# Forward substitution steps on VectorE moved behind the addition to x, in a gated delta-net and feed-forward kernel on one Trainium2 core

## Chip, core and metric

The kernel runs on one core of one Trainium2 chip. A core has five engines that run side by side and wait for each other through semaphores: PE (TensorE, matmuls; its weight loads are listed apart as PEld), DVE (VectorE), ACT (ScalarE), POOL (GpSimd) and SP (SyncE, which here issues the DMAs). The metric is the device time of one execution in microseconds (us), the median of several. A profile is one execution that the hardware profiler recorded.

## What is computed

The input x has 4 sequences of 1024 tokens of width 256. Two layers follow one another, each as x + layernorm(layer(layernorm(x))): a gated delta-net attention with 32 value heads of width 128 (16 query/key heads, each for two value heads), and a feed-forward layer whose weights are looked up in a table of 16 values. Nearly all the time goes into the first. Cut to what matters, for each head and each chunk of 64 tokens:

```python
mixed = silu(conv4(x @ W_qkv))                 # q, k, v; q and k are then normalised
A = -(k_beta @ k.T * decay) * strict           # 64x64, strictly lower triangular
Tm = solve_triangular(eye - A, eye)            # its inverse, by forward substitution
u, kcd = Tm @ v_beta, Tm @ (k_beta * exp(g))
# over the 16 chunks in order, St is the state (128x128):
v_new = u - kcd @ St
out = (q * exp(g)) @ St + attn @ v_new
St = St * exp(g_last) + (k * exp(g_last - g)).T @ v_new
```

The output of a head is then normalised, gated with silu(x @ W_z) and projected with W_out.

## The kernel before

**Tiling.** Two sequences and one chunk make a tile of 128 rows (`p` is the pair of sequences, 0 or 1). Four heads are worked on together (a group; there are eight), and a group's 32 tiles are cut into four super-blocks of eight units. A unit is one tile with four heads. There are 256 units in 32 super-blocks. Consecutive units belong to the two pairs in turn, so the state that a unit reads was last changed two units before.

**The slots.** The order of the work is written out by hand. Each pass of the loop of line 871 is a slot: it carries one unit through the recurrence, and does a share of the work for later super-blocks and for the output of earlier units. The strings of `SLOTS` (lines 858 to 867) give the order of issue, one string for each value of `iq` from 0 to 7; I call them slot 0 to slot 7. Each word resumes a generator up to its next `yield`:

- `A` and `B` (`channel`, line 389): the projection and the four-tap convolution of a channel tile of v (A) and of q or k (B). PE writes PSUM (L422), ACT takes the first tap (L436), DVE adds the other three into the tile `cv` (L439), ACT applies silu (L443). The convolution's later parts are put off by a few words through a list of due work (`go`, line 821). A step `v` doesn't count in that list.
- `N0`, `N1`, `N2`, `O3`, `O4`, `J` (`step`, line 657): the recurrence of a unit. N0 transposes v (L670) and scales it into x0 (L674). N1 multiplies k and q with the state (`pkqs`, L683), and **adds to x** on DVE (L694, four instructions; the profile calls the tile x). N2 applies the diagonal inverse to it on PE (`px`, L703), makes `xs` (ACT, L708) and `yg` (DVE, L711), and has POOL decay the state (L720). In the next slot O3 multiplies with the attention (`po`, L703) and adds on DVE (`core`, L727), J squares on ACT (L732), and O4 multiplies into `pu` (L740) and **adds to the state** S on DVE (L747). So a slot's O3, J and O4 belong to one unit and its N1 and N2 to the next one.
- `Z`, `T`, `U` (`project_out`, line 768): the gate `pz` on PE (L142), its silu `zs` on ACT (L781), two multiplications of `zs` on POOL (L783, L785), a transpose and `pout` on PE (L789, L796), and an addition `ac` on DVE (L801).
- `n` (`norms`), `r` and `q` (`rms`, with three small DVE instructions at L753 to L762, and `roots`), `s` (`scores`: POOL L529, L530 and L536, ACT L533, PE `kkq` L545, DVE L555), `b` (`build`).
- After each O4, POOL also does a piece of the feed-forward layer's table lookup (`lut_pieces`, L300 and L304).
- `v1`, `v2`: one or two **steps of the forward substitution** (`invert`, line 563; lines 897 to 900). The inverse of the 32x32 diagonal blocks of a super-block (128 blocks, one to a partition) takes 31 steps of two DVE instructions, a product `rank` (L579) and a subtraction from `v` (L580). Step j works on (j+1)(31-j) elements a partition: 31 at both ends, 256 in the middle. A first call of the generator only loads `lb` and clears `v`; the last one also stores `v` to DRAM. The substitution of a super-block starts in slot 4 and runs through 5, 6, 7, 0 and 1; what is left in slot 2 is drained there.

```python
    for j in range(BS - 1):
        w = BS - 1 - j
        sh = [P, j + 1, w]
...
        V.tensor_tensor(t, bc(v[:, 0 : j + 1, j : j + 1], sh), bc(lb[:, j : j + 1, j + 1 :], sh), ALU.mult)
        V.tensor_tensor(v[:, 0 : j + 1, j + 1 :], v[:, 0 : j + 1, j + 1 :], t, ALU.subtract)
```

**What the engines share.** The PSUM tiles come from two rings. One has two buffers of two banks (`psum2`), taken in turn by A's `pp`, `pu` and B's `pp`, so that a slot's `pu` takes the buffer that B's `pp` of the slot before held, and waits until DVE has read it out (L439). The other has four banks (`psum`) for everything else. Each engine takes its instructions in the order of issue. The two instructions of a step have both inputs in SBUF; L694, L747, L711, L727, L555 and L439 have one input in PSUM.

Of the kernel before, what the change touches and what calls it, by code (L numbers as in the profile page):

```python
# [14 lines left out]
B, S, HID = 4, 1024, 256  # L15
# [48 lines left out]
def delta_net_ffn_kernel(  # L64
# [18 lines left out]
    V, A, G_, T_ = nc.vector, nc.scalar, nc.gpsimd, nc.tensor  # L83
# [84 lines left out]
    def layer_norm_stats(pool, src, n, tag):  # L168

        mv = pool.tile([P, n, 2], F32, tag=f"mv{tag}", name=f"mv{tag}")  # L170
        for i in range(n):
            st = pool.tile([P, 6], F32, tag=f"st{tag}", name=f"st{tag}")
            V.bn_stats(st, src(i))
            V.bn_aggr(mv[:, i, :], st)
        r = pool.tile([P, n], F32, tag=f"r{tag}", name=f"r{tag}")
        G_.tensor_scalar_add(r, mv[:, :, 1], LN_EPS)
        G_.tensor_tensor(r, r, bc(rsqrt, [P, n]), ALU.pow)
        return mv, r
# [14 lines left out]
    with tc.tile_pool(name="pre", bufs=2) as pre, tc.tile_pool(name="gates", bufs=1) as gp:  # L193
# [13 lines left out]
        for s in range(NSB):  # L207
# [4 lines left out]
            mv, r = layer_norm_stats(pre, lambda i: xt[:, i, :], SB, "a")  # L212
# [95 lines left out]
    with ExitStack() as main:  # L308
# [533 lines left out]
        def work(kind, n, *args):  # L842
# [13 lines left out]
        LQ = 2 * SB + 5  # L856
        LV = SB // 2
        SLOTS = [
            "A v1 O3 s N0 v1 T n J O4 v1 N1 Z v1 B n N2 U n s",
            "A v1 O3 N0 v1 T J v1 O4 N1 r Z v1 B N2 q s U",  # L860
            "A v1 O3 N0 v1 T J v1 O4 v1 N1 Z s v1 B N2 n U",
            "b A O3 N0 T J O4 N1 Z s B N2 U b",
            "v1 A b O3 s N0 v1 T n J O4 v1 N1 Z v1 B n N2 v1 U n s",
            "A v1 O3 N0 v1 T J v1 O4 v1 N1 r Z v1 B N2 q s v1 U",
            "A v1 O3 N0 v1 T J v1 O4 v1 N1 Z s v1 B N2 n v1 U",
            "A v1 O3 N0 v1 T J v1 O4 v1 N1 Z s v1 B N2 v1 U",
        ]

        units = [(k, u) for k in supers for u in range(SB)]
        with tc.manual_schedule(engines=COMPUTE):  # L870
            for s in range(-LQ, len(units)):
                n, i = divmod(s, SB)
# [58 lines left out]
    with tc.tile_pool(name="fw", bufs=1) as fw, tc.tile_pool(name="fs", bufs=2) as fs:  # L931
# [7 lines left out]
        for s in range(NSB):  # L939
# [6 lines left out]
            mv, r = layer_norm_stats(fs, lambda i: acb[:, i, :], SB, "b")  # L946
# [3 lines left out]
            mv, r = layer_norm_stats(fs, lambda i: xt[:, i, :], SB, "c")  # L950
# [32 lines left out]
            mv, r = layer_norm_stats(fs, lambda i: acb[:, i, :], SB, "d")  # L983
# [57 lines left out]
```

## Time and profile before

| | |
|---|---|
| time, median of 3 runs | 4435.06 us (4429.75 to 4438.18) |
| the profiled execution | 4434.46 us, of it a span of 4432.7 us |
| busy in the span: PE, PEld | 91%, 65% |
| busy in the span: DVE, ACT, POOL | 79%, 60%, 47% |
| granted PE clock, mean | 0.968 |
| L579 `rank`, 992 instructions | 468.2 us, 472 ns each |
| L580 `v`, 992 instructions | 555.0 us, 559 ns each |
| POOL L783, L785 (256 each), L720 (224) | 1041, 1283, 1947 ns each |

In a line of a timeline stand the start and the duration in us, the engine, the line of the kernel, the operation, the tile written and the tiles read, the shapes, and in brackets the idle time before it with what ended it. In a table of stretches each engine's busy time stands beside the length of the stretch. The chain of waits is followed back from the last instruction, at each step to what released it or to the instruction before it on its engine.

### The profile page before, as it was taken

What the parts mean: (1) busy time and instruction counts of PE and PEld (TensorE: products, weight loads), DVE (VectorE), ACT (ScalarE), POOL (GpSimd) and SP (SyncE); (2) the same over time, 40 slices, a digit from 0 to 9 for tenths busy, and PEclk for the clock granted to TensorE, in tenths of its full rate; (3) what the DMA queues carried; (4) which work ended last, traced back from release to release, by engine and by line L of the source; (5) the groups of instructions that cost most, each with busy time, mean ns of one, the idle gap of its engine ahead of it and who ended that gap; (6) DMA issues with size and microseconds to landing.
All of it is one profiled execution on the core that took longest, in us unless ns stands there. A gap on an engine that the chain in (4) does not pass through costs nothing.

```text
span 4432.7 us, 79363 instructions
## 1 busy us (share of the span) xinstructions
PE 4021.3 (91%) x26664; PEld 2876.3 (65%) x26664; DVE 3514.5 (79%) x6641; ACT 2646.0 (60%) x6573; POOL 2069.1 (47%) x1752
## 2 busy tenths in 40 slices
PE   3679999999999999999999999999999999995888
PEld 3456766676767766677667676776766666673444
DVE  4788888888888888888888888889888888861442
ACT  2466666666666666666666666666666666662111
POOL 2545554655555555554455555555453334331221
PEclk7899999999999999999999999999999999997999
DMA  3444444544454444444444445444444444432110
GB/s 94 114 116 110 106 120 118 133 117 114 129 135 125 118 121 132 114 116 127 126 130 118 115 127 135 125 116 118 126 119 117 123 126 120 102 84 72 36 33 19
DMA packets 1052418, 492.70 MB, mean 111 GB/s; under 512 B 729824, under 2 KB 951152, under 8 KB 1052016
## 3 DMA queue, kind: packets, MB, share of 16 engines
q1 hardware_dynamic: 1052016, 487.64, 42.0%
q8 instruction: 216, 3.54, 0.3%
q14 instruction: 186, 1.52, 0.1%
HBM read 267.66 MB, written 219.69 MB: 110 GB/s over the span
## 4 chain that ended last, share of the span: by engine, by line
PE 59%; DVE 24%; issue 6%; ACT 6%; POOL 3%; DMA 2%; SPq 1%; DVEq 0%; POOLq 0%; ACTq 0%
PE pp L422 13%; DVE cv L439 8%; PE pout L796 7%; PE pz L142 7%; PE pkqs L683 7%; PE px L703 4%; DVE rank L579 4%; PE pu L740 4%; PE po L703 3%; PE pgu L963 3%; PE py L975 2%; DVE v L580 2%; PE kkq L545 2%; PE pto L789 2%; PE pv L670 1%
## 5 line engine op out<-in xcount | busy, mean ns | idle before, releaser
L439 DVE SCALAR_TENSOR_TENSOR cv<-pp,cw,cv 128x512 f32<-128x512 f32 x1536 | 1148.8, 748 | 356.6 <-ACT cv L436 327.2
L783 POOL TENSOR_TENSOR zs<-zs,rr 128x512 f32<-128x512 f32 x256 | 266.4, 1041 | 1586.6 <-ACT zs L781 1577.6
L436 ACT ACTIVATE cv<-pp,cw 128x512 f32<-128x512 f32 x512 | 350.7, 685 | 489.3 <-PE pp L422 489.3
L580 DVE TENSOR_TENSOR v<-v,rank 128x31 f32<-128x31 f32 (+15 forms) x992 | 555.0, 559 | 34.1
L422 PE MATMUL pp<-xnT,wq 128*128 128x262 f32 x2048 | 532.1, 402 | 43.8 <-DVE cv L439 35.1
L796 PE MATMUL pout<-wo,oT 128*128 128x256 f32 x2048 | 512.0, 395 | 8.1 <-ACT oT L791 8.1
L422 PEld LDWEIGHTS pp<-xnT,wq 128*128 128x128 f32 x2048 | 372.7, 192 | 217.1 <-issue 59.6
L422 PE MATMUL pp<-xnT,wv 128*128 128x262 f32 x2048 | 502.5, 387 | 6.1 <-DVE cv L439 6.1
L142 PE MATMUL pz<-wzs,xnT 128*64 128x512 f32 x2048 | 488.8, 598 | 4.7 <-DVE ac L801 3.8
L579 DVE TENSOR_TENSOR rank<-v,lb 128x31 f32<-128x31 f32 (+15 forms) x992 | 468.2, 472 | 24.5 <-DMA lb<-ltd 18.8
L683 PE MATMUL pkqs<-S,qku 128*64 128x256 f32 x3840 | 476.8, 387 | 4.2 <-DVE core L727 2.5
L720 POOL TENSOR_TENSOR S<-S,dkm 128x1024 f32<-128x1024 f32 x224 | 436.2, 1947 | 26.0 <-PE pkqs L683 26.0
L703 PE MATMUL px<-x,ue 128*128 128x128 f32 x2048 | 296.1, 289 | 157.5 <-issue 102.2
L703 PEld LDWEIGHTS px<-x,ue 128*128 128x128 f32 x2048 | 266.9, 196 | 258.0 <-issue 147.7
L422 PEld LDWEIGHTS pp<-xnT,wv 128*128 128x128 f32 x2048 | 381.4, 190 | 74.1 <-issue 13.4
L796 PEld LDWEIGHTS pout<-wo,oT 128*128 128x128 f32 x2048 | 388.2, 200 | 56.3 <-ACT oT L791 10.0
L683 PEld LDWEIGHTS pkqs<-S,qku 128*64 128x64 f32 x3840 | 249.2, 136 | 201.4 <-issue 51.0
L732 ACT ACTIVATE junk<-core 128x128 f32<-128x128 f32 x1024 | 318.8, 311 | 66.7 <-DVE core L727 38.4
L785 POOL TENSOR_TENSOR zs<-zs,core 128x512 f32<-128x512 f32 x256 | 328.4, 1283 | 20.1
L708 ACT ACTIVATE xs<-px 128x512 f32<-128x512 f32 x256 | 154.4, 603 | 237.5 <-PE px L703 237.4
L740 PE MATMUL pu<-yg,kt 64*128 64x256 f32 x1920 | 272.2, 402 | 15.4 <-DVE cv L439 14.0
L300 POOL TENSOR_SCALAR lt<-lx,lutb 128x344 f32<-128x344 int32 (+2 forms) x210 | 276.6, 1317 | 16.9
(166 smaller groups left out, 7081.7 us busy)
## 6 DMA issues: line engine op xcount, KB each, us to landing
qkd<-qk SPq DMA_DIRECT2D x256, 256.0 KB, 2.5
qku<-qkd SPq DMA_DIRECT2D x256, 256.0 KB, 2.9
dc<-rows_d SPq DMA_DIRECT2D x256, 128.0 KB, 3.4
ltd<-lT SPq DMA_DIRECT2D x128, 256.0 KB, 2.5
atd<-aT SPq DMA_DIRECT2D x128, 256.0 KB, 2.8
ae<-atd SPq DMA_DIRECT2D x512, 64.0 KB, 2.6
acc_d<-ac SPq DMA_DIRECT2D x256, 128.0 KB, 2.2
ac<-acc_d SPq DMA_DIRECT2D x224, 128.0 KB, 2.6
```

The costliest lines, as they stand in the source:

```text
L142: T_.matmul(ps[ab * C : (ab + 1) * C, :], lhsT=xnT[:, kc, 2 * p + ab, H + n * C : H + (n + 1) * C], rhs=rhs(kc), start=kc == 0, stop=kc == ...
L422: T_.matmul(ps[:, 2 * p : 2 * p + 2, : H + BT], lhsT=wt[:, kc, :], rhs=xnT[:, kc, 2 * p : 2 * p + 2, c0 : c0 + H + BT], start=kc == 0, sto ...
L436: A.activation(cv, ps[:, :, H : H + BT], AF.Copy, scale=cw[:, ch, H : H + 1])
L439: V.scalar_tensor_tensor(cv, ps[:, :, i : i + BT], cw[:, ch, i : i + 1], cv, ALU.mult, ALU.add)
L579: V.tensor_tensor(t, bc(v[:, 0 : j + 1, j : j + 1], sh), bc(lb[:, j : j + 1, j + 1 :], sh), ALU.mult)
L580: V.tensor_tensor(v[:, 0 : j + 1, j + 1 :], v[:, 0 : j + 1, j + 1 :], t, ALU.subtract)
L683: T_.matmul(as4(ps)[ab * C : (ab + 1) * C, two, :], lhsT=qk[:, m, j, ab, :], rhs=S_[:, ab, two, :], start=True, stop=True,)
L703: T_.matmul(as4(ps)[:, h, :], lhsT=w[:, h, :], rhs=src[:, h, :], start=True, stop=True)
L720: G_.tensor_tensor(flat, flat, bc(decay, [P, 2 * HG, P]), ALU.mult)
L740: T_.matmul(as4(pu[:, ab])[:, two, :], lhsT=kt[half, m, :], rhs=yg[half, two, :], start=True, stop=True)
L785: G_.tensor_tensor(zs, zs, k.cores.pop(u), ALU.mult)
L796: T_.matmul(pp[:, :HID], lhsT=oT[:, h, :], rhs=wo[:, h, :], start=h == 0, stop=h == HG - 1)
```

## The change

The strings of the slots alone change. No step `v` stands any more between J and O4 (slots 1, 2, 5, 6 and 7), and none between O4 and N1 (slots 0, 2, 4, 5, 6 and 7). They stand behind N1: two in slots 1, 2, 4, 5, 6 and 7, one in slot 0. In slot 4 a step that stood behind Z is one of the two. The number of steps in a slot stays, but in slot 1, which has five in place of four, so that the last of the 31 steps falls into slot 1 and no longer into slot 2. All other engines keep their order of issue, and so do all DVE instructions but the steps.

```diff
         SLOTS = [
-            "A v1 O3 s N0 v1 T n J O4 v1 N1 Z v1 B n N2 U n s",
-            "A v1 O3 N0 v1 T J v1 O4 N1 r Z v1 B N2 q s U",
-            "A v1 O3 N0 v1 T J v1 O4 v1 N1 Z s v1 B N2 n U",
+            "A v1 O3 s N0 v1 T n J O4 N1 v1 Z v1 B n N2 U n s",
+            "A v1 O3 N0 v1 T J O4 N1 v2 r Z v1 B N2 q s U",
+            "A v1 O3 N0 v1 T J O4 N1 v2 Z s v1 B N2 n U",
             "b A O3 N0 T J O4 N1 Z s B N2 U b",
-            "v1 A b O3 s N0 v1 T n J O4 v1 N1 Z v1 B n N2 v1 U n s",
-            "A v1 O3 N0 v1 T J v1 O4 v1 N1 r Z v1 B N2 q s v1 U",
-            "A v1 O3 N0 v1 T J v1 O4 v1 N1 Z s v1 B N2 n v1 U",
-            "A v1 O3 N0 v1 T J v1 O4 v1 N1 Z s v1 B N2 v1 U",
+            "v1 A b O3 s N0 v1 T n J O4 N1 v2 Z B n N2 v1 U n s",
+            "A v1 O3 N0 v1 T J O4 N1 v2 r Z v1 B N2 q s v1 U",
+            "A v1 O3 N0 v1 T J O4 N1 v2 Z s v1 B N2 n v1 U",
+            "A v1 O3 N0 v1 T J O4 N1 v2 Z s v1 B N2 v1 U",
         ]
```

## The prediction

> **What bounds the kernel now.** I read the page first, then the busy time by slot, then the timelines of one super-block. The page calls it a PE kernel.
>
> ```profile
> PE 4021.3 (91%) x26664; PEld 2876.3 (65%) x26664; DVE 3514.5 (79%) x6641; ACT 2646.0 (60%) x6573; POOL 2069.1 (47%) x1752
> ...
> PE 59%; DVE 24%; issue 6%; ACT 6%; POOL 3%; DMA 2%; SPq 1%; DVEq 0%; POOLq 0%; ACTq 0%
> ```
>
> But DVE holds 24% of the chain, and the slots differ. The stretches below run from one `po` to the next: slots 5, 6, 7 and 0 of one super-block.
>
> ```profile
> core 0: us, PE busy (x) PEld busy (x) DVE busy (x) ACT busy (x) POOL busy (x), PEclk, DMA share, GB/s
> ...
> 2041.04:2058.72 17.68, 15.06 (x83) 11.02 (x82) 17.12 (x33) 11.24 (x27) 9.57 (x9) 0.90 0.36 83
> 2058.72:2073.99 15.27, 14.10 (x99) 10.63 (x98) 14.96 (x25) 9.81 (x25) 9.91 (x9) 1.00 0.26 69
> 2073.99:2089.45 15.46, 14.11 (x99) 10.62 (x98) 15.11 (x29) 7.71 (x22) 5.49 (x4) 1.00 0.56 169
> 2089.45:2104.08 14.63, 14.63 (x96) 10.22 (x94) 12.83 (x30) 9.64 (x26) 4.56 (x4) 1.00 0.47 129
> ```
>
> In slots 5 to 7 DVE is busy for all but 0.56, 0.31 and 0.35 us, which is its gaps between instructions, and PE is idle for 2.62, 1.17 and 1.35 us. **DVE bounds these three slots.** In slot 0 PE is busy throughout. So what the change does to DVE's time decides slots 5 to 7, and not how early x comes.
>
> Slot 7, on DVE:
>
> ```profile
> 2080.16 0.42 DVE L579 TENSOR_TENSOR rank<-v,lb 128x247 f32<-128x247 f32 x1
> 2080.61 0.42 DVE L580 TENSOR_TENSOR v<-v,rank 128x247 f32<-128x247 f32 x1
> 2080.95 1.22 DVE L747 TENSOR_TENSOR S<-pu,S 128x1024 f32<-128x1024 f32 x1
> 2082.08 0.83 DVE L579 TENSOR_TENSOR rank<-v,lb 128x240 f32<-128x240 f32 x1
> 2082.95 1.35 DVE L580 TENSOR_TENSOR v<-v,rank 128x240 f32<-128x240 f32 x1
> 2084.22 1.11 DVE L694 SCALAR_TENSOR_TENSOR x<-pkqs,dkm,x 128x128 f32<-128x128 f32 x4
> 2085.26 0.67 DVE L555 TENSOR_TENSOR lT<-kkq,dc 128x512 f32<-128x512 f32 x1
> ...
> 2086.46 0.38 DVE L579 TENSOR_TENSOR rank<-v,lb 128x231 f32<-128x231 f32 x1
> 2086.87 0.40 DVE L580 TENSOR_TENSOR v<-v,rank 128x231 f32<-128x231 f32 x1
> ```
>
> POOL in the same slot, and PE:
>
> ```profile
> 2081.61 1.04 POOL L783 TENSOR_TENSOR zs<-zs,rr 128x512 f32<-128x512 f32 x1 [8.95 <-ACT zs L781]
> 2082.73 1.31 POOL L785 TENSOR_TENSOR zs<-zs,core 128x512 f32<-128x512 f32 x1
> 2084.00 2.06 POOL L720 TENSOR_TENSOR S<-S,dkm 128x1024 f32<-128x1024 f32 x1
> 2086.04 1.14 POOL L300 TENSOR_SCALAR lw<-lx,lutb 128x256 f32<-128x256 int32 x1
> ```
>
> ```profile
> 2084.77 1.13 PE L703 MATMUL px<-x,ue 128*128 128x128 f32 x8 [1.35 <-DMA ac<-acc_d]
> ```
>
> Two things are to be seen. First, `px` waits 1.35 us for x, and two steps stand ahead of x (the releaser named is not the real one; x's first quarter ends at 2084.22+0.34). Second, the step at 2082.08 takes 2.22 us where its neighbours take 0.81 to 0.87: its `rank` ends at 2082.91, 0.26 us after POOL's L783 (2082.65), and its `v` at 2084.30, 0.26 us after L785 (2084.04). **A step's instruction waits while one of these POOL instructions runs.** L694 at 1.11 us and L555 at 0.67 us run beside POOL's L720 at their usual length. They read PSUM.
>
> **The change, part by part.** No instruction is added or removed. What counts is where the steps meet POOL.
>
> *POOL's block stays where it is.* L783 follows ACT's zs, which follows ACT's silu of `cv` and `qs`; the three POOL instructions run without a gap. None of what they wait for moves in DVE's order, and the steps never stood ahead of that `cv`.
>
> *Slot 7.* The step of 2080.16 goes from ahead of S, which starts there; x follows 1.13 us behind the start of S (slot 2, where no step stands between: 2123.89 and 2125.02), so it runs from 2081.29 to 2082.40. PE's wait at `px` goes. Then come four step instructions in a row, and the block is in its first 1.04 us. The first ends at 2082.91 and the second at 2084.30, as before. The third waits for the end of L720 (2084.00 + 2.06 = 2086.06) and ends near 2086.3, the fourth 0.4 later; L555 starts near 2086.65 in place of 2085.26. DVE is **1.4 us later**: before, x and L555 filled the time of L720; now a step waits it out.
>
> *Slot 6.* The same from its rows: S from 2064.36, x to 2066.6, block from 2066.12 to 2070.59, fourth instruction to 2071.3, L555 at 2071.2 in place of 2069.80: **1.4**.
>
> *Slot 5.* S from 2047.68, x to 2049.9, block 2049.32 to 2053.67, fourth instruction to 2054.3, so 1.33 later. But behind it stands `eq` (L753), which took 0.82 us beside L720 and takes 0.16 alone: 0.67. One more step meets L536 at the end of the slot in place of another, perhaps -0.3 (estimate from steps of 0.8 and 1.6 us there). **0.4**.
>
> *What of it ends late.* 3.2 us on DVE in a super-block. PE first takes up its slack: B's last `cv` in slot 7 ended at 2088.45 + 1.53 = 2089.98, and `pu`, which needs that buffer, started at 2091.31, so 1.33 us are free; slot 0's `px` has about 1.0. I take 1.2. After that PE waits at `pu` where it waited at `px`. **2.0 us** a super-block.
>
> *Slot 1.* Here only the step ahead of O4 moves, and the last step comes over from slot 2. Before, `eq` and `rr` met the block:
>
> ```profile
> 2112.61 1.27 DVE L753 TENSOR_SCALAR eq<-n 128x8 f32<-128x8 f32 x1
> 2113.99 1.75 DVE L754 SCALAR_TENSOR_TENSOR rr<-ms,eq 128x16 f32<-128x16 f32 x1
> ```
>
> They already waited out L785 and L720 (to 2115.71). Now the two steps do, and `rr`, with the extra step of 0.4 us, comes behind: B's `cv` starts near 2117.1 in place of 2116.27, 0.85 late; its end at 2119.06 had 0.05 us to `pu` (2119.11). In slot 2, PE's `pkqs` waited for `core` behind the step that is now gone (1.43 us), which gives some 0.35 back. **0.5 us**.
>
> *At nothing:* slot 0 (the step sat alone at 0.65 us ahead of x, and POOL's block starts at 2099.44, after it either way; `px` has slack; if the cover went, 0.65 us), slot 4 (steps of 60 and 87 elements, 0.47 and 0.52 us, in a slot with 7 us of DVE idle), slots 2 and 3 (no steps left to run). The last step's store of `v`, on SP, comes a few us earlier; its readers run in slot 3. The steps issue no other DMA.
>
> *Count.* 31 super-blocks have their steps beside units. In the first of each of the eight groups the units of slots 5 and 6 have no state yet, hence no x and no L720; there only slot 7 counts, 1.4 - 1.2 = 0.2. Sum: 23 x 2.0 + 8 x 0.2 + 31 x 0.5 = 46 + 2 + 16 = 64 us on the profiled execution's 4434.5 us, which is 0.6 us from the median: **4498 us**, 1.4% slower.
>
> *A rule of the skill.* The rows show steps held by TENSOR_TENSOR on POOL, but the steps at 2086.46 and 2086.87 ran at 0.38 and 0.40 us beside L300, a TENSOR_SCALAR from 2086.04 to 2087.18. The Trainium skill, "SBUF — State Buffer", section "SBUF: two separate sides", calls the pair that VectorE and GpSimd share an exclusive lock: a VectorE instruction with two SBUF inputs and a GpSimd one that reads SBUF block each other for a whole instruction. That speaks against this change, and it would let L300 block too, which the row denies. By the rule, the fourth instruction would often wait out L300 behind L720 as well, up to 1.1 us in slots 6 and 7, an estimate of up to 50 us more. I go by the row.
>
> **Rivals.** *Faster (14%):* the steps cost no more in the new place, since POOL comes late or lets both steps in between its instructions. Then DVE's time stays and what stood between `px` and `pu` is gained, 1.2 us: 31 x 1.2 = 37 us, **4398 us**. If DVE were not the bound after all, all PE waits of slots 5 to 7 would go: 23 x 5.1 + 8 x 1.35 = 128 us, 4306 us. For it: PE does wait for x. Against: DVE's columns. It decides as soon as DVE's added time in slots 5 to 7 falls under 1.2 us, of 3.2.
>
> *No change (9%):* the added waits are about 1.2 us a super-block and the slack takes them: **4435 us**.
>
> *Much slower (12%):* no slack, as PE now waits at `pu`, at `ac` and at `cv` in turn, slot 1 in full, and a further 0.8 us from steps that meet other POOL work: 23 x 4.0 + 8 x 1.4 + 31 x 0.85 = 130 us, **4564 us**. That the change didn't do what it says can't be: the order of issue is the order on DVE.
>
> **The numbers.** The forecast (65%) spans 4465 to 4535 by its own terms (1.0 to 1.5 us a slot, slack 0.9 to 1.33). The range leaves out the faster cases and what lies beyond the much slower one: 4440 to 4565. A difference under 0.2% can't be told from none here. Faster 0.14, same 0.09, slower 0.77.
>
> **What would show it.** In the profile after: `px` without its wait in slots 5 to 7 (right for the first step); steps behind x of 1 to 2 us an instruction that end just after L783, L785 and L720, and L579 and L580 with higher means than 472 and 559 ns; L753 short; new PE waits at `pu`, `pto` or `pp` for `cv` and `yg`. I am wrong if the step instructions behind x stay near 0.4 us, or if DVE shows idle time in slots 5 to 7.

## Result and profile after

The changed kernel takes 4553.53 us (median of 4 runs, 4551.29 to 4558.39), beside 4435.91 us for the kernel before (median of 4, 4429.75 to 4438.18). The ratio is 1.0269, with a 95% interval of 1.0251 to 1.0287: **117.6 us slower**. The forecast had 64 us. The time lies inside the stated range of 4440 to 4565, but above the 4465 to 4535 that the forecast spans by its own terms, and near the rival "much slower" (130 us). The executions compared in the profiles lie 124 us apart.

The profile after, from its page: the chain that ended last, and the two groups of the steps.

```profile
DVE 43%; PE 35%; ACT 11%; issue 6%; DMA 2%; POOL 2%; SPq 1%; DVEq 0%; ACTq 0%; POOLq 0%
...
L579 DVE TENSOR_TENSOR rank<-v,lb 128x31 f32<-128x31 f32 (+15 forms) x992 | 584.3, 589 | 31.2 <-DMA lb<-ltd 23.4
L580 DVE TENSOR_TENSOR v<-v,rank 128x31 f32<-128x31 f32 (+15 forms) x992 | 581.4, 586 | 34.3 <-DVE rank L579 0.2
```

PE had 59% of the chain and DVE 24%; now DVE leads. The same 1984 step instructions took 1023.2 us together and now take 1165.7.

The timeline of a slot 7, DVE first, then POOL's block in the same slot:

```profile
2027.23 0.41 DVE L579 TENSOR_TENSOR rank<-v,lb 128x252 f32<-128x252 f32 x1
...
2028.02 1.22 DVE L747 TENSOR_TENSOR S<-pu,S 128x1024 f32<-128x1024 f32 x1
2029.15 1.12 DVE L694 SCALAR_TENSOR_TENSOR x<-pkqs,dkm,x 128x128 f32<-128x128 f32 x4
2030.19 0.69 DVE L579 TENSOR_TENSOR rank<-v,lb 128x247 f32<-128x247 f32 x1
2030.91 1.37 DVE L580 TENSOR_TENSOR v<-v,rank 128x247 f32<-128x247 f32 x1
2032.32 1.99 DVE L579 TENSOR_TENSOR rank<-v,lb 128x240 f32<-128x240 f32 x1
2034.34 0.57 DVE L580 TENSOR_TENSOR v<-v,rank 128x240 f32<-128x240 f32 x1
```

```profile
2029.57 1.04 POOL L783 TENSOR_TENSOR zs<-zs,rr 128x512 f32<-128x512 f32 x1 [10.49 <-ACT zs L781]
2030.69 1.32 POOL L785 TENSOR_TENSOR zs<-zs,core 128x512 f32<-128x512 f32 x1
2031.98 2.06 POOL L720 TENSOR_TENSOR S<-S,dkm 128x1024 f32<-128x1024 f32 x1
```

Read the ends. The first three step instructions behind x end at 2030.88, 2032.28 and 2034.31; POOL's three end at 2030.61, 2032.01 and 2034.04. Each step instruction ends 0.27 us after a POOL instruction. The third takes 1.99 us, where its like at 2027.23 takes 0.41. In the same slot on PE, with the idle time before each in brackets:

```profile
2030.09 1.05 PE L703 MATMUL px<-x,ue 128*128 128x128 f32 x8
...
2036.16 0.66 PE L670 MATMUL pv<-ident,vt 128*128 128x128 f32 x4 [0.42 <-DVE aT L555]
2038.25 0.63 PE L789 MATMUL pto<-ident,zs 128*128 128x128 f32 x4 [1.43 <-DVE yg L711]
2039.61 2.08 PE L740 MATMUL pu<-yg,kt 64*128 64x256 f32 x8 [0.73 <-DVE cv L439]
```

`px` no longer waits, but PE stands 2.58 us a little later, for `aT`, `yg` and `cv`, which DVE hands over late. Over the whole run PE's longest waits are now these, where they were for `px` (102.2 us with the releaser put down as issue, 39.0 us with ACT's cv):

```profile
PE pto L789 <- DVE yg L711: 121.1, 102, 1.9
PE pu L740 <- DVE cv L439: 84.5, 118, 2.5
```

To see where the 118 us lie, I take the time from the end of one `core` (L727) to the end of the next, by slot, from both traces: medians, and the mean of 30 of each, which holds also the super-blocks at a group's start.

| from `core` of slot | 0 | 1 | 2 | 3 | 4 | 5 | 6 | 7 | sum |
|---|---|---|---|---|---|---|---|---|---|
| before, median us | 14.50 | 14.20 | 12.12 | 16.28 | 16.57 | 16.40 | 15.64 | 15.20 | 120.92 |
| after, median us | 14.51 | 13.79 | 13.52 | 16.28 | 16.57 | 16.55 | 17.05 | 16.81 | 125.08 |
| after less before, mean us | +0.25 | -0.38 | +1.36 | -0.02 | 0.00 | +0.18 | +0.85 | +1.55 | +3.80 |

3.80 us on the mean, 31 times, is 118 us. Slots 5 to 7 give 2.58 of them, slots 1 and 2 together 0.98, slot 0 0.25.

### The profile page after: what moved, and what is told of

It is laid out like the page before. It is cut to its first block, busy times and chain, and to the rows that moved or that the text cites. A ratio compares the mean times of both kernels' runs of the same rounds, so it can differ in the third digit from the quotient of the medians.

```text
span 4556.3 us, 79381 instructions
## 1 busy us (share of the span) xinstructions
PE 4080.2 (90%) x26664; PEld 2888.7 (63%) x26664; DVE 3599.0 (79%) x6641; ACT 2650.9 (58%) x6573; POOL 2071.5 (45%) x1752
## 4 chain that ended last, share of the span: by engine, by line
DVE 43%; PE 35%; ACT 11%; issue 6%; DMA 2%; POOL 2%; SPq 1%; DVEq 0%; ACTq 0%; POOLq 0%
DVE cv L439 13%; DVE rank L579 9%; PE pp L422 7%; DVE v L580 6%; PE pz L142 5%; PE pout L796 4%; PE pkqs L683 4%; PE pgu L963 2%; DVE S L747 2%; DVE x L694 2%; PE py L975 2%; PE px L703 2%; DVE core L727 2%; PE pu L740 2%; PE po L703 2%
## 5 line engine op out<-in xcount | busy, mean ns | idle before, releaser
L439 DVE SCALAR_TENSOR_TENSOR cv<-pp,cw,cv 128x512 f32<-128x512 f32 x1536 | 1148.8, 748 | 388.4 <-ACT cv L436 359.0
L783 POOL TENSOR_TENSOR zs<-zs,rr 128x512 f32<-128x512 f32 x256 | 266.5, 1041 | 1692.1 <-ACT zs L781 1692.1
L579 DVE TENSOR_TENSOR rank<-v,lb 128x31 f32<-128x31 f32 (+15 forms) x992 | 584.3, 589 | 31.2 <-DMA lb<-ltd 23.4
L580 DVE TENSOR_TENSOR v<-v,rank 128x31 f32<-128x31 f32 (+15 forms) x992 | 581.4, 586 | 34.3 <-DVE rank L579 0.2
L683 PE MATMUL pkqs<-S,qku 128*64 128x256 f32 x3840 | 507.8, 408 | 12.7 <-DVE ac L801 7.6
L796 PE MATMUL pout<-wo,oT 128*128 128x256 f32 x2048 | 495.8, 386 | 8.5 <-ACT oT L791 7.8
L720 POOL TENSOR_TENSOR S<-S,dkm 128x1024 f32<-128x1024 f32 x224 | 436.3, 1948 | 26.9 <-PE pkqs L683 26.9
L683 PEld LDWEIGHTS pkqs<-S,qku 128*64 128x64 f32 x3840 | 264.2, 145 | 232.0 <-issue 57.5
L796 PEld LDWEIGHTS pout<-wo,oT 128*128 128x128 f32 x2048 | 374.5, 193 | 55.0 <-ACT oT L791 9.6
L443 ACT ACTIVATE qk<-cv 128x512 f32<-128x512 f32 x256 | 161.4, 630 | 394.6 <-DVE cv L439 389.4
L740 PE MATMUL pu<-yg,kt 64*128 64x256 f32 x1920 | 297.6, 432 | 84.9 <-DVE cv L439 84.5
L785 POOL TENSOR_TENSOR zs<-zs,core 128x512 f32<-128x512 f32 x256 | 328.8, 1285 | 20.1
L703 PE MATMUL px<-x,ue 128*128 128x128 f32 x2048 | 279.2, 279 | 8.1 <-issue 2.5
```

Of the source, the lines that this page charges most:

```text
L439: V.scalar_tensor_tensor(cv, ps[:, :, i : i + BT], cw[:, ch, i : i + 1], cv, ALU.mult, ALU.add)
L683: T_.matmul(as4(ps)[ab * C : (ab + 1) * C, two, :], lhsT=qk[:, m, j, ab, :], rhs=S_[:, ab, two, :], start=True, stop=True,)
L703: T_.matmul(as4(ps)[:, h, :], lhsT=w[:, h, :], rhs=src[:, h, :], start=True, stop=True)
L720: G_.tensor_tensor(flat, flat, bc(decay, [P, 2 * HG, P]), ALU.mult)
L740: T_.matmul(as4(pu[:, ab])[:, two, :], lhsT=kt[half, m, :], rhs=yg[half, two, :], start=True, stop=True)
L785: G_.tensor_tensor(zs, zs, k.cores.pop(u), ALU.mult)
```

## Experiments

All times are medians. Kernels that were measured together share one set of runs of the kernel before, so its time differs a little from one group to the next.

**1 and 2: the two parts by themselves.** The strings of `SLOTS` are taken from the one kernel or the other:

```diff
-            "A v1 O3 N0 v1 T J v1 O4 v1 N1 r Z v1 B N2 q s v1 U",
-            "A v1 O3 N0 v1 T J v1 O4 v1 N1 Z s v1 B N2 n v1 U",
-            "A v1 O3 N0 v1 T J v1 O4 v1 N1 Z s v1 B N2 v1 U",
+            "A v1 O3 N0 v1 T J O4 N1 v2 r Z v1 B N2 q s v1 U",
+            "A v1 O3 N0 v1 T J O4 N1 v2 Z s v1 B N2 n v1 U",
+            "A v1 O3 N0 v1 T J O4 N1 v2 Z s v1 B N2 v1 U",
```

This is the first; the second has the change's other four strings and these three as before.

> The kernel before with the new strings in slots 5, 6 and 7 alone. Theory (POOL's block of three TENSOR_TENSORs holds the steps, and DVE is what these slots end on): about +88 us on the kernel before, from the slots' lengths in the two traces (+0.2, +0.9, +1.6 and +0.2 us on the mean in slots 5, 6, 7 and 0, 31 times), so some 4523 us. Rival (the loss is spread by the lower granted clock, or sits in slots 0 to 2 by what comes late there): well under 60 us.

> The other part alone: new strings in slots 0, 1, 2 and 4, those of before in 5, 6 and 7. Theory: slots 1 and 2 give 1.0 us together where the prediction had 0.5, because rms comes behind the two held steps and ACT's chain behind it; +30 us, some 4466 us, and the two parts add up to the whole 118. Rival (the two parts only hurt together, since slot 0 starts late): near 0.

Measured beside 4431.8 us: 4526.1 us (ratio 1.0212, 1.0197 to 1.0227) for slots 5 to 7, and 4469.4 us (1.0084, 1.0060 to 1.0109) for the others. So 94 and 38 us, both near what the slots' lengths gave, and the loss is where the table puts it. The mean granted clock is lower in the first run too (0.959 in its profile, 0.968 in the one before), so its time alone doesn't rule out the clock. The slots do: in the profile after, slots 6 with and without a spell of lower clock both take 17.05 us, and slots 7 16.81 with and 16.88 without (medians). The parts add up to 132 us and not 118; the second's interval alone is 22 us wide, and what the difference is stays open.

**3 and 4: without POOL's block.** Both orders without L783, L785 and L720.

```diff
-            G_.tensor_tensor(zs, zs, bc(k.rr[u // 4][:, u % 4, :].unsqueeze(2), h4), ALU.mult)
-            G_.tensor_tensor(zs, zs, k.cores.pop(u), ALU.mult)
+            k.cores.pop(u)
...
-                    G_.tensor_tensor(flat, flat, bc(decay, [P, 2 * HG, P]), ALU.mult)
+                    pass
```

> The kernel before without POOL's L783, L785 and L720: it leaves out the scaling by rr, the product with core and the decay of the state, so its output is another one. To be read beside the next run only. Theory: steps near 0.4 us an instruction also behind the addition to S; DVE has less to do in slots 5 to 7, some 4 us less a super-block, so 100 us or more under the kernel before.

> The changed kernel without the same three POOL instructions (the same work left out). Theory: nothing holds the steps behind x any more, so it is within 15 us of the run before this one, or faster, since x comes earlier. Rival (the order itself costs, because DVE hands yg, cv and ac to PE later): the 118 us between the two orders stay, at least 60 of them.

4262.2 us in the old order (0.9616, 0.9602 to 0.9631) and **4250.1 us in the new one** (0.9588, 0.9574 to 0.9603). The 118 us between the orders are gone, and the new one is 12 us ahead. The order itself costs nothing; it costs where the block stands. From the page of the new order without the block:

```profile
L579 DVE TENSOR_TENSOR rank<-v,lb 128x31 f32<-128x31 f32 (+15 forms) x992 | 367.0, 370 | 37.4 <-DMA lb<-ltd 22.9
```

370 ns each, from 589.

**5 and 6: why PE's slack brought nothing.** In the table slot 0 keeps its 14.50 us, where the prediction had PE take up 1.2. The chain of waits of the profile after runs through that slot like this:

```profile
2044.79 1.04 ACT sq L468 x2
...
2048.45 0.49 ACT zs L781
2048.93 0.59 ACT cv L436
```

DVE's `cv` for A ends at 2044.14, then ACT does vt, two squares of norms, four of the unit, qs, zs and B's first tap, and DVE goes on with B's `cv` at 2049.55. The chain goes on over POOL. POOL's block starts behind `zs`, at 2049.01, and L529 and L530 of the scores follow it without a gap; on DVE, two instructions ahead of the next `core` wait for them:

```profile
2053.22 1.04 POOL L529 TENSOR_TENSOR dc<-dc,dkm 128x512 f32<-128x512 f32 x1
2054.34 1.30 POOL L530 TENSOR_TENSOR dc<-dc,above 128x512 f32<-128x512 f32 x1
```

```profile
2053.36 0.93 DVE L501 SCALAR_TENSOR_TENSOR ncd<-cc,dkm 128x16 f32<-128x16 f32 x1
...
2054.54 1.26 DVE L580 TENSOR_TENSOR v<-v,rank 128x135 f32<-128x135 f32 x1
2055.72 0.68 DVE L727 TENSOR_TENSOR core<-po,qs 128x512 f32<-128x512 f32 x1
```

Without POOL's block (run 4) these two take 0.17 and 0.30 us. The same stands in the profile before:

```profile
2103.78 0.94 DVE L501 SCALAR_TENSOR_TENSOR ncd<-cc,dkm 128x16 f32<-128x16 f32 x1
...
2104.96 1.25 DVE L580 TENSOR_TENSOR v<-v,rank 128x135 f32<-128x135 f32 x1
```

In both kernels, the last super-block apart, `zs` ends 7.04 us behind `core` in slot 0, and where `px` isn't late (see the last section) the next `core` ends 7.46 us behind `zs`: together 14.50.

To shorten the part on ACT, the squares of norms go ahead, into a gap of ACT:

```diff
-            "A v1 O3 s N0 v1 T n J O4 N1 v1 Z v1 B n N2 U n s",
+            "A v1 O3 s n N0 v1 T J O4 N1 v1 Z v1 B n N2 U n s",
```

and the same in the kernel before, with its own steps.

> The changed kernel with slot 0's first norms step (two squares on ACT, 1.04 us) moved from between T and J to ahead of N0. Theory: slot 0 ends on a chain from DVE's cv over ACT (vt, squares, junk, qs, zs, cv) back to DVE, 14.50 us from core to core in both kernels, which is why PE's slack brought nothing; with 1.04 us less of it, slot 0 of the changed kernel gets shorter by up to 1.0 us, less where PE's half clock falls into it: -10 to -31 us on the changed kernel's 4553.5, so 4522 to 4543 us. Rival (slot 0 ends on PE's own work): no change, 4549 to 4558 us.

> The kernel before with the same move. Theory: there PE is just as long as that chain in slot 0 (14.63 us of PE in 14.63), so it gains nothing or a few us: 4420 to 4436 us. Rival (the squares bind in both): -31 us.

The first came to 4545.3 us beside 4432.9 (1.0255, 1.0241 to 1.0269), 8 us under the changed kernel's 4553.5, less than expected, and the two intervals overlap. The slot itself shows it: where no spell of PE's clock at half speed (see the last section) began shortly ahead of its `px`, slot 0 went from 14.50 to 13.94 us (medians of 12 and 13), as `zs` came 0.55 us earlier. The 17 slots with such a spell have a median of 15.01 us, and eight of them took 16.3, so the mean of slot 0 fell by only 0.09. The second came to 4420.8 us (0.9975, 0.9967 to 0.9984): 12 us faster. There too slot 0 shrank, to 13.95, while slot 0's `px` stayed where it was (6.61 us behind `core` in both), and slot 1 took most of it back, 14.73 from 14.20; on the mean the two together went from 28.70 to 28.40 us. So in slot 0 two chains of nearly the same length stand side by side, PE's and the one over ACT and POOL, in the kernel before as well, and the prediction saw only PE's.

**7: rms first in slot 1.**

```diff
-            "A v1 O3 N0 v1 T J O4 N1 v2 r Z v1 B N2 q s U",
+            "A v1 O3 N0 v1 T J O4 N1 r v2 Z v1 B N2 q s U",
```

> The changed kernel with r ahead of the two steps in slot 1. Theory: the 1.0 us that slots 1 and 2 lose comes from rr, which stands behind two steps that POOL's block holds, and from ACT's chain behind rr (square root, two table loads, exponentials, cv); with rr ahead of them slot 2 starts its cv earlier: -0.4 to -0.9 us a super-block, 4526 to 4541 us. Rival (it is PE's wait at pu for B's cv, which still stands behind the steps): within 8 us of 4553.5.

4535.2 us beside 4432.9 (1.0232, 1.0218 to 1.0246): 18 us under the changed kernel, as expected, and slot 2 went from 13.52 to 12.99 us. In the changed kernel, DVE and then ACT at that place:

```profile
2062.48 1.29 DVE L579 TENSOR_TENSOR rank<-v,lb 128x60 f32<-128x60 f32 x1
2063.80 1.82 DVE L580 TENSOR_TENSOR v<-v,rank 128x60 f32<-128x60 f32 x1
```

```profile
2066.31 0.22 ACT L764 ACTIVATE rr<-rr 128x16 f32<-128x16 f32 x1 [0.75 <-DVE rank L579]
```

The step of 60 elements (0.47 us alone) takes 3.1 us against L785 and L720. `rr` comes behind it, ACT's square root waits 0.75 us, and behind the square root stand two table loads and two exponentials, then the first tap of A in slot 2.

**8: the decay in another form.** The same products on POOL, as TENSOR_SCALARs:

```diff
-                    G_.tensor_tensor(flat, flat, bc(decay, [P, 2 * HG, P]), ALU.mult)
+                    for i in range(2 * HG):
+                        G_.tensor_scalar_mul(flat[:, i, :], flat[:, i, :], decay[:, i, :])
```

> The changed kernel with the decay of the state (L720) as eight TENSOR_SCALARs of 128x128 in place of one TENSOR_TENSOR of 128x1024; the same arithmetic, POOL busy for longer. Theory by the row of L300 (steps beside a TENSOR_SCALAR run at their usual length): the third and fourth step instruction behind x in slots 6 and 7 take 0.4 us in place of 2.0 and 0.6; slots 5 to 7 lose 1 to 2 us each, and the kernel is 60 to 110 us under the changed one, 4445 to 4495 us. Rival by the rule of the skill's page (every POOL instruction that reads SBUF holds them): each of the two waits for one of the eight, 0.6 to 0.9 us an instruction, and less than half of that gain.

4402.3 us beside 4431.7 (0.9936, 0.9919 to 0.9952): 151 us under the changed kernel, more than expected, and faster than the kernel before, though POOL takes 5.09 us for the eight where L720 took 2.06. In a slot 7 the second step behind x, and L555:

```profile
1958.35 0.46 DVE L579 TENSOR_TENSOR rank<-v,lb 128x240 f32<-128x240 f32 x1
1958.84 0.55 DVE L580 TENSOR_TENSOR v<-v,rank 128x240 f32<-128x240 f32 x1
1959.32 0.68 DVE L555 TENSOR_TENSOR lT<-kkq,dc 128x512 f32<-128x512 f32 x1
```

Beside the eight (1958.02 to 1963.11) the step takes 0.97 us from start to L555, where the same step took 2.51 in the profile after. It isn't quite free: the median of this step (240 elements) is 1.04 us, and 0.85 where nothing runs beside it. By the lengths from `core` to `core`, though, slots 5 to 7 gave less than the 3 to 6 us forecast for them: 1.48 of the 4.98 us a super-block, on the mean. Slot 0 gave 1.86, slot 4 1.37 and slot 1 0.65, and slot 2 lost 0.39. In slot 0 `zs` ends 7.04 us behind `core` as before, but `ncd` takes 0.17 and the step's `v` 0.35 us, and the slot takes 13.04.

**9 and 10: the steps behind the block.** On the kernel before, the step between O4 and N1 and the one behind Z go behind N2, and `r` in slot 5 too. The steps ahead of S stay.

```diff
-            "A v1 O3 N0 v1 T J v1 O4 v1 N1 r Z v1 B N2 q s v1 U",
-            "A v1 O3 N0 v1 T J v1 O4 v1 N1 Z s v1 B N2 n v1 U",
-            "A v1 O3 N0 v1 T J v1 O4 v1 N1 Z s v1 B N2 v1 U",
+            "A v1 O3 N0 v1 T J v1 O4 N1 Z B N2 r v2 q s v1 U",
+            "A v1 O3 N0 v1 T J v1 O4 N1 Z s B N2 v2 n v1 U",
+            "A v1 O3 N0 v1 T J v1 O4 N1 Z s B N2 v3 U",
```

> The kernel before with the contended step of slots 5, 6 and 7 moved behind N2, so behind the block and behind B's cv, and the one behind Z with it; in slot 5 r moves there too. The steps ahead of S stay. Theory: no step meets POOL's block, DVE falls under PE's 14.1 us in these slots, and PE's waits of 2.6, 1.2 and 1.35 us at px go: 90 to 150 us under the kernel before, some 4310 us. Rival (the order and not the block makes the time, as in the changed kernel, where x came early too): at or over 4435 us.

> The kernel with the steps behind N2 in slots 5 to 7 (c1) and the early squares of slot 0. Theory: the two gains add, 12 us under c1, some 4321 us. Rival: PE bounds slot 0 there and nothing is gained, 4333 us.

c1 takes **4333.0 us beside 4432.9** (0.9779, 0.9766 to 0.9793), 100 us faster than the kernel before and 220 faster than the changed one. With the early squares, c2 takes 4326.4 beside 4431.7 (0.9762, 0.9748 to 0.9777); the 7 us between them are within their intervals. DVE in a slot 6 of c1, where POOL's block ran from 1902.60 to 1906.85:

```profile
1902.75 1.12 DVE L694 SCALAR_TENSOR_TENSOR x<-pkqs,dkm,x 128x128 f32<-128x128 f32 x4
...
1906.24 1.53 DVE L439 SCALAR_TENSOR_TENSOR cv<-pp,cw,cv 128x512 f32<-128x512 f32 x2
1907.68 0.41 DVE L579 TENSOR_TENSOR rank<-v,lb 128x252 f32<-128x252 f32 x1
1908.13 0.42 DVE L580 TENSOR_TENSOR v<-v,rank 128x252 f32<-128x252 f32 x1
```

Beside the block stand only instructions that read PSUM (x, L555, L439, L711), at their usual lengths, and the steps come after it.

## Why the prediction was right, and where its size was off

**What bounds slots 5 to 7: right.** DVE's time decided them, not x. x came earlier in all three, `px` lost its wait, and the slots grew. With the block left out, the same order was faster (4250 beside 4262).

**POOL's block holds the steps: right, in place and in size.** The first three step instructions behind x end just after L783, L785 and L720, as the prediction had them one by one: by slot and instruction 0.20 to 0.28 us after on the median, and each within 0.4 us in at least 22 of the 24 slots 5 that have the block, 22 of the 24 slots 6 and 30 of the 32 slots 7. The forecast was 0.4, 1.4 and 1.4 us for slots 5, 6 and 7, 3.2 together; from `core` to `core` the medians grew by 0.15, 1.41 and 1.61, 3.17 together. The mean of 2.58 holds also the first super-blocks of the groups, which the prediction counted apart.

**The slack of 1.2 us: wrong, and this is the failed term.** The prediction let PE take up 1.2 us in slot 0 and came to 2.0 us a super-block. PE did take it up: where its clock stayed whole, `px` came 5.33 us behind `core`, and 6.61 before. But the next `core` came 14.50 us later in both: DVE waits there for ACT, and then `ncd` and a step wait for POOL's L529 and L530. The slack was read on PE alone; the chain from DVE over ACT and POOL back to DVE had none. Run 8 shows that POOL's part counts: with ACT as late as before and the two DVE instructions not held, slot 0 takes 13.04. The prediction put slot 0 at nothing because POOL's block comes after its step in either order; but the POOL instructions that follow that block hold the later one. 1.2 us in 31 super-blocks are 37 of the missing 54 us. On top of it, `px` came late in more of the slots 0 (below), and their mean grew by 0.25 us, 8 us in all: 12 of 30 took over 15.5 us, and 5 of 30 before.

**Slot 1: the mechanism right, half the size.** Forecast 0.5 us, measured 0.98 over slots 1 and 2. The prediction followed B's `cv` to `pu`, and missed that `rr`, behind the two held steps, stands ahead of a chain on ACT that ends at A's `cv` of slot 2. With `rr` ahead of the steps, 18 us of some 30 came back. The missing half is another 15 us; slots 5 to 7 stayed some 5 us under their forecast.

**What cost nothing: right.** Slots 3 and 4 kept their lengths to 0.02 us.

**Rule against row: the row.** Steps beside TENSOR_SCALARs keep nearly their length, 1.04 us a step beside the eight of run 8 where 0.85 is usual. What the Trainium skill, "SBUF — State Buffer", section "SBUF: two separate sides", states of the shared pair agrees with the TENSOR_TENSORs here and is too wide for the TENSOR_SCALARs.

**The rival that decides at 1.2 us** was told from the forecast by the added time in slots 5 to 7: 3.2 us, far from it. The "much slower" rival named no slack and slot 1 in full, and both held; its further 0.8 us from other POOL work didn't come in slots 5 to 7.

## What to carry to other kernels

When instructions of two SBUF inputs on DVE are moved, lay POOL's TENSOR_TENSORs beside them and see which they meet; fill the time of those with DVE instructions that read PSUM. A wait that goes elsewhere is only moved. An engine's busy time alone doesn't say that it decides a slot: in a slot 0 of the profile after, PE was busy in 14.33 of 14.50 us, and the slot ended on the other chain. Before a term of slack is put in, look for a second chain of the same length through the other engines, here through ACT and POOL.

## What the runs showed of the hardware

PE's granted clock fell to half in spells of 3.41 us, some of 6.83 (12 of the 31 counted below). One of 3.41 us in the profile after came behind the waits of 0.42, 1.43 and 0.73 us shown above:

```profile
2040.00:2041.00 1.00, 1.00 (x6) 0.79 (x6) 0.97 (x4) 1.00 (x4) 0.00 (x0) 0.50 0.20 33
```

The clock is the number after POOL's busy time: 0.50. `pu` took 2.08 us there, and 1.14 with the clock whole. Between `px` of slot 7 and `px` of slot 0 there were 3 such spells of 20 in the profile before, counted from the tenth unit on, and 18 of 31 in the one after; the others lie between `px` of slot 4 and `px` of slot 7. In the profile after, slots 0 with one took 15.57 us and slots without 14.50 (medians). In runs 1 and 7 the median of slots 0 with such spells is 14.51, like that of the others. What tells them apart is when `px` comes: in these three profiles and the one before, slots 0 whose `px` starts by 6.97 us behind `core` took at most 14.52 us, and those whose `px` starts at 7.62 or later took 15.55 to 15.63. In the longer ones of the profiles before and after, the step's `v` ends behind the second L529 and not behind the first L530, 1.06 us later.

Between two POOL instructions that follow without a gap, one step instruction gets through in the slots shown. It ends 0.26 to 0.27 us after the first of them with 240 or 247 elements, 0.16 us after with 135 (slot 0) and 0.08 us after with 60 (slot 1). So three POOL instructions hold three step instructions, however short those are: the step of 60 elements took 3.1 us in place of 0.47.
